# Feed-forward transposes moved from TensorE to VectorE squares and DMA, with the next input loaded most of a block sooner

## The chip, the cores and the metric

The kernel runs on one core of a Trainium2 chip. The metric is the device time of one execution, in microseconds (us). Five engines work side by side: TensorE (PE, matrix products), VectorE (DVE), ScalarE (ACT), GpSimd (POOL) and SyncE (SP), which here issues the transfers (DMAs). They meet through semaphores. SBUF is the working memory with 128 partitions; PSUM holds what PE produces.

## The reference

64 sequences of 64 tokens with 256 features (x, 4096 tokens in all) pass through four layers. Each has parameters that depend on a condition vector of the sequence (cond, 64 numbers).

- Layer 0: an up projection with GELU gate, quantised activations and ternary weights.
- Layer 1: attention with 16 heads and a gated feed-forward part, each behind a conditional root-mean-square norm:
```
x = x + a_alpha * _attention(_ada_rmsnorm(x, t, gamma, beta), W_q, W_k, W_v, W_o)
return x + f_alpha * _swiglu(_ada_rmsnorm(x, t, gamma, beta), gate_w, hidden_w, out_w, out_b)
# _ada_rmsnorm: (t @ gamma_w.T) * x * rsqrt(mean(x*x) + eps) + (t @ beta_w.T)
# _swiglu: silu(x @ gate_w.T) * (x @ hidden_w.T) @ out_w.T + out_b, with 1024 hidden units
```
- Layer 2: a layer norm over the 256 features with weight, bias and a conditional term.
- Layer 3: an adapter with matrices of its own for each sequence, 256 to 128 and back:
```
down = relu(einsum('bld,bnd->bln', x, Wd + dWd[b]) + bd)
return x + einsum('bln,bdn->bld', down, Wu + dWu[b]) + bu
```
The change lies in the stretch that computes the feed-forward part of layer 1, layer 2 and layer 3.

## The kernel before

The 4096 tokens are 8 blocks (i = 0 to 7) of 512 tokens, each 4 tiles of 128. Layer 0 and the attention come first; the sum after the attention, x2, is written to DRAM (x2d). The last loop, `for n in range(5, N)`, begins at about 447 us of the span. Step n is block i = n // 8 and part f = n % 8: 128 of the 1024 hidden units. Products of full precision are made from a high and a low half (three matmuls, mm3, L83 to L85).

A block has two layouts. Token-major has 128 tokens on the partitions: there the norms' means are taken and the residual is added. Feature-major has 128 features on the partitions (two chunks c of 256): products need their input so. The turn from the first to the second happens at two places of the loop, and PE makes it, as four transposes of 128 x 128 into a PSUM bank each time:

- norm_turn, for the normed input xn of the next block, chunk c at f = 5 and 6. Transposes (L256), then DVE multiplies by gamma (xg, L259), POOL adds beta (L260), and one step later split makes the halves xh (ACT, L239) and xl (POOL, L240).
- f_adapt, for the layer norm's output x3 of the block before, chunk c at f = 4 and 5. Transposes (L913), then DVE makes x4 (L914), the adapter's input.

One step of the loop, in order: f_inner (PE: gate and value products into two banks; ACT: silu, L796; DVE: their product sg, L799); the pieces of other blocks; f_parts (ACT: high half hhi, L836; DVE: low half hlo, L837); f_outer for the step two before (PE: acc += h x wout, L83 to L85).

The pieces of other blocks, by f: 0: the load of x2 of block i+1 (f_load, fx, L759, 512 KB). 1: its squares (f_begin: ACT junkf L232, POOL root L223 and L225); of block i-1 acc times alpha plus x2 (f_scaled L859, f_added L864) and its statistics. 2: f_center (DVE nm L876, ACT x3 L878); the rows of alpha and out_b for block i (f_rows, L271, four transfers). 3: f_scale, xn from x2 and the root (ACT xnf, L247). 6: the load of the adapter's down matrices wd (L890, four transfers). 7: of wu (L894, four); f_down of block i-1 (PE L943, ACT Relu dn L947); f_up of block i-2 (PE L959 in two chunks, DVE yo L975, store out_y L977); on POOL f_common (the shared part of wd, L904) and f_base (x2 plus out_b, L780).

PSUM has eight banks here: four with the tag gh, two mm, two acc. At f = 7 the mm banks are taken in the order up chunk 0, down, up chunk 1, so up chunk 1 takes the bank that yo of up chunk 0 reads. Of the SBUF tiles that count here, x1 (x2 and x3 of a block) has five buffers, xn one, xh and xl two each, x4 two, dn and yo one.

Order: PE, ACT, DVE and POOL follow the order in which the program is written (`tc.manual_schedule`). SP's transfers are placed by a planner. Every transfer on SP also waits for the one that stands eight before it.

Of the kernel before, what the change touches and what calls it, by code (L numbers as in the profile page):

```python
# [8 lines left out]
F32 = mybir.dt.float32  # L9
# [3 lines left out]
ALU = mybir.AluOpType  # L13
# [4 lines left out]
P = 128  # L18
NB = 64
L = 64  # L20
D = 256
NTOK = NB * L
T = 512
NBLK = NTOK // T
BB = T // L
TT = T // P
# [6 lines left out]
V_NORM, V_AG, V_AB, V_AA, V_FG, V_FB, V_FA, V_LIN = range(8)  # L33
# [3 lines left out]
def tile_kernel(ctx: ExitStack, tc, xT, x, condT, cw, upT, downT, qkvT, woT, ghT, outT_w,  # L37
                vecs, rows, g1, g2, gb, out):
    nc = tc.nc
# [3 lines left out]
    main = ctx.enter_context(tc.tile_pool(name="main", bufs=1))  # L43
# [8 lines left out]
    pools = {}  # L52
# [7 lines left out]
    uid = [0]  # L60

    def bank(tag):
        uid[0] += 1
        tags = pools["tags"]
        if tag not in tags:
            tag = "mm"
        return pools["ps"].tile([P, 512], F32, tag=tag, bufs=tags[tag], name=f"{tag}_{uid[0]}")
# [19 lines left out]
    def b3(ap):  # L87
        return ap.rearrange("p (b l) -> p b l", l=L)
# [19 lines left out]
    E = mybir.EngineType  # L108
    engines = {E.PE, E.Activation, E.DVE, E.Pool}
    ordered = ExitStack()  # L110
# [19 lines left out]
    def bc(v, c, i, bs=slice(0, BB)):  # L130

        n = bs.stop - bs.start
        return cv[:, v, c, i * BB + bs.start:i * BB + bs.stop].unsqueeze(2).broadcast_to([P, n, L])
# [87 lines left out]
    def rsqrt(ss, scale, eps, name, n=TT):  # L221
        ms = main.tile([P, TT], F32, tag="ms", bufs=2, name=f"ms_{name}")
        nc.gpsimd.tensor_scalar(ms[:, :n], ss, scale, eps, ALU.mult, ALU.add)  # L223
        rs = main.tile([P, TT], F32, tag="rs", bufs=2, name=f"rs_{name}")
        nc.gpsimd.tensor_tensor(rs[:, :n], ms[:, :n], nhalf[:, :n], ALU.pow)  # L225
        return rs
# [11 lines left out]
    def split(hl, c, xs, eng=None):  # L238
        nc.scalar.copy(hl[0][:, c], xs)  # L239
        (eng or nc.vector).tensor_tensor(hl[1][:, c], xs, hl[0][:, c].bitcast(F32), ALU.subtract)  # L240
# [11 lines left out]
    def norm_turn(xn, hl, i, c, vg, vb):  # L252

        pt = bank("mm")
        for t in range(TT):
            nc.tensor.transpose(pt[:, t * P:(t + 1) * P], xn[:, t, c * P:(c + 1) * P], ident)  # L256
        uid[0] += 1
        xg = main.tile([P, T], F32, tag="xg", bufs=2, name=f"xg{uid[0]}")
        nc.vector.tensor_tensor(b3(xg), b3(pt), bc(vg, c, i), ALU.mult)  # L259
        nc.gpsimd.tensor_tensor(b3(xg), b3(xg), bc(vb, c, i), ALU.add)  # L260
        return lambda: split(hl, c, xg, nc.gpsimd)

# [494 lines left out]
    def f_load(i):  # L757
        x2 = block(f"fx2_{i}")
        nc.sync.dma_start(out=x2, in_=tok(x2d, i))  # L759
        fblk[i] = dict(x2=x2)  # L760

    def f_begin(i):
        fblk[i]["rs"] = rms(fblk[i]["x2"], f"f{i}")

    def f_scale(i):
        fblk[i]["n"] = norm_tm(fblk[i]["x2"], fblk[i]["rs"], f"f{i}", True)
# [26 lines left out]
    def f_inner(n):  # L793
        pg, pv = f_products(n)
        sg = main.tile([P, T], F32, tag="st", bufs=2, name=f"sg{n}")
        nc.scalar.activation(sg, pg, AF.Silu)  # L796
        if n == LAST:
            return sg, pv
        nc.vector.tensor_tensor(sg, pv, sg, ALU.mult)  # L799
        return sg  # L800
# [15 lines left out]
    def f_parts(n, sg):  # L816
        pool = pools["b"]
        if n in KEPT:

            if n == KEPT[0]:  # L820
                fun["kept"] = parts("kept")
            h_hi, h_lo = (k[:, n - KEPT[0]] for k in fun["kept"])
        else:
            h_hi = pool.tile([P, T], F32R, tag="oh", bufs=3, name=f"hhi{n}")
            h_lo = pool.tile([P, T], F32R, tag="ol", bufs=3, name=f"hlo{n}")
        fun[n] = (h_hi, h_lo)
        if n == LAST:
            sg, pv = sg
            halves = [slice(k * T // 2, (k + 1) * T // 2) for k in range(2)]
            for k in halves:  # L830
                nc.vector.tensor_tensor(sg[:, k], pv[:, k], sg[:, k], ALU.mult)
                nc.scalar.copy(h_hi[:, k], sg[:, k])
            for k in halves:
                nc.vector.tensor_tensor(h_lo[:, k], sg[:, k], h_hi[:, k].bitcast(F32), ALU.subtract)  # L834
            return
        nc.scalar.copy(h_hi, sg)  # L836
        nc.vector.tensor_tensor(h_lo, sg, h_hi.bitcast(F32), ALU.subtract)  # L837
# [69 lines left out]
    def f_adapt(i, c):  # L907
        B = fblk[i]
        if c == 0:
            B["x4"] = pools["c"].tile([P, 2, T], F32, tag="x4", bufs=2, name=f"x4_{i}")  # L910
        pt = bank("mm")
        for t in range(TT):
            nc.tensor.transpose(pt[:, t * P:(t + 1) * P], B["x3"][:, t, c * P:(c + 1) * P], ident)  # L913
        nc.vector.scalar_tensor_tensor(b3(B["x4"][:, c]), b3(pt), w2[:, c:c + 1], bc(V_LIN, c, i),  # L914
                                       ALU.mult, ALU.add)

    def f_turn(i, k):
# [16 lines left out]
    def f_down(i, half=None):  # L934
        B = fblk[i]
        if half in (None, 0):
            B["dn"] = pools["c"].tile([P, T], F32, tag="dn", bufs=1, name=f"dn{i}")
        b0, b1 = (0, BB) if half is None else (half * BB // 2, (half + 1) * BB // 2)
        pd = bank("mm" if half is None else "acc")
        for b in range(b0, b1):  # L940
            for c in range(2):
                for s in range(2):
                    nc.tensor.matmul(pd[s * 64:(s + 1) * 64, (b - b0) * L:(b - b0 + 1) * L],  # L943
                                     lhsT=B["wd"][b // 4][:, b % 4, c, s * 64:(s + 1) * 64],
                                     rhs=B["x4"][:, c, b * L:(b + 1) * L], start=c == 0, stop=c == 1,
                                     tile_position=(0, 64 * s))
        nc.scalar.activation(B["dn"][:, b0 * L:b1 * L], pd[:, :(b1 - b0) * L], AF.Relu, bias=vc[:, 5, 0:1])  # L947
# [211 lines left out]
    bias = pools["bias"] = pools["c"].tile([P, 2, D], F32, name="bias")  # L1159
    gbt = pools["c"].tile([P, 4, D], F32, tag="yo", bufs=1, name="gbt")  # L1160
    nc.sync.dma_start(out=gbt, in_=gb)
    late = []
    for n in range(5, N):
        i, f = divmod(n, 8)
        more = i + 1 < NBLK

        for rest in late:
            rest()
        late = []
        if i > 0 and f == 2:  # L1170
            f_added(i - 1, 1)
            f_stats(i - 1, 1)
            rln = rsqrt(fblk[i - 1]["mv"][:, :, 1], 1.0, 1e-5, f"ln{i - 1}")
        sg = f_inner(n)
        if i > 0 and f in (4, 5):
            f_adapt(i - 1, f - 4)
        if more and f in (5, 6):
            late = [norm_turn(*fblk[i + 1]["n"], i + 1, f - 5, V_FG, V_FB)]
        up = i - 2 if more and f == 7 else i - 2 if not more and f == 0 else -1
        if up >= 0:  # L1180

            def between(pus):
                f_up_store(up, pus, chunks=range(1))
                if more:
                    f_down(i - 1)
            pus = f_up_products(up, between=between)
            f_up_store(up, pus, chunks=range(1, 2))
        elif more and i > 0 and f == 7:
            f_down(i - 1)
        f_parts(n, sg)  # L1190
        if n > 5:
            f_outer(n - 2, range(2 if n - 2 in KEPT else TT))
        if n == 6:
            for k in range(2):
                nc.vector.scalar_tensor_tensor(bias[:, k], gbt[:, 2 * k + 1], 0.1, gbt[:, 2 * k], ALU.mult, ALU.add)
        if i > 0:
            if f == 1:
                for k in range(2):
                    f_scaled(i - 1, k)
                f_added(i - 1, 0)  # L1200
                f_stats(i - 1, 0)
            if f == 2:
                f_center(i - 1, range(TT), rln)
        if i > 0 and more:
            if f == 0:
                f_load(i + 1)
            if f == 1:
                f_begin(i + 1)
            if f == 3:
                f_scale(i + 1)  # L1210
        if f == 2 and i > 0:
            f_rows(i)

        if f == (6 if more else 1):
            f_weights(i, "wd")
        if f == (7 if more else 1):
            f_weights(i, "wu")
        if more and f == 7:
            f_common(i, "wd", 0)
            f_base(i)  # L1220
        if i > 0 and f == 0:
            f_common(i - 1, "wd", 1)
        if i > 0 and f in (3, 4):
            f_common(i - 1, "wu", f - 3)
        if not more:
            if f == 4:
                f_base(i)
            if f in (5, 6):
                f_common(i, "wd", f - 5)
                f_common(i, "wu", f - 5)  # L1230
# [57 lines left out]
```

## Time and profile before

| | |
|---|---|
| time, median of 3 runs | 748.66 us (748.53 to 748.88) |
| the profiled execution | 748.95 us, span 746.8 us |
| last loop, f = 0 of block 1, 2, 3, 4, 5, 7 on PE | 458.95, 496.41, 535.73, 575.08, 614.47, 693.07 us |
| DMA traffic over the span | 159 GB/s on average |

Times in the profile are us from the start of the span unless marked ns. A group line reads: line, engine, operation, out<-in, shapes, count, then busy time and mean ns of one instruction, then the idle time before them with what ended it. A timeline line reads: start, duration, engine, line, operation, out<-in, shapes, count, and in brackets the idle time just before with its releaser. SPq marks the issue of transfers: its time is the time on SP, not until the data land. PEclk is the clock that TensorE was granted, as a share of full speed.

The shares of the chain that ended last, by engine:

```profile
PE 61%; DVE 17%; ACT 11%; issue 5%; DMA 3%; POOL 2%; SPq 1%; DVEq 0%; ACTq 0%; POOLq 0%
```

Most of what the end waited for is PE's own work.

### The profile page before, as it was taken

How to read it: one execution, taken by the hardware profiler on the slowest of the kernel's cores; microseconds unless marked ns; L12 is line 12 of the kernel's file. 1: busy time of each engine (PE TensorE's matmuls, PEld its weight loads, DVE VectorE, ACT ScalarE, POOL GpSimd, SP SyncE). 2: the span in 40 equal slices, each digit the busy share in tenths (PEclk: the TensorE clock that was granted, in tenths of full speed). 3: DMA queues.
4: the chain of work that ended last, by engine and by line, in shares of the span. 5: the costliest groups of instructions: out<-in, count | busy, mean ns of one | idle time of the engine just before them, and what ended most of it. 6: DMA issues, size and time to landing. Idle time of an engine off the chain costs nothing.

```text
span 746.8 us, 17456 instructions
## 1 busy us (share of the span) xinstructions
PE 734.7 (98%) x7036; PEld 612.1 (82%) x7036; DVE 542.2 (73%) x843; ACT 405.6 (54%) x849; POOL 340.4 (46%) x359
## 2 busy tenths in 40 slices
PE   9999999999999999999999999999999999999997
PEld 8866766777686878888888888888888888888886
DVE  4998878867687698889888876646555555565676
ACT  5553445335435588998888674535253434434242
POOL 2123133133134426765655427464646464545292
PEclk9999999999999999999999999999999999999999
DMA  8897999999995866444655237623261709080821
GB/s 258 244 265 171 270 280 231 300 278 261 229 273 108 195 153 162 113 134 122 164 150 129 79 101 183 148 52 91 63 163 32 196 4 224 1 198 2 222 62 58
DMA packets 117456, 118.87 MB, mean 159 GB/s; under 512 B 39632, under 2 KB 101200, under 8 KB 117376
## 3 DMA queue, kind: packets, MB, share of 16 engines
q1 hardware_dynamic: 109232, 91.29, 49.6%
q0 software_dynamic: 7488, 25.37, 10.9%
q10 hardware_dynamic: 656, 1.11, 0.5%
q8 instruction: 55, 0.90, 0.5%
q14 instruction: 25, 0.20, 0.1%
HBM read 71.41 MB, written 29.56 MB: 135 GB/s over the span
## 4 chain that ended last, share of the span: by engine, by line
PE 61%; DVE 17%; ACT 11%; issue 5%; DMA 3%; POOL 2%; SPq 1%; DVEq 0%; ACTq 0%; POOLq 0%
PE mm L83 9%; PE mm L85 8%; PE mm L84 8%; PE gh L85 4%; PE gh L84 4%; PE gh L83 4%; PE mm L476 3%; PE mm L298 3%; PE acc L83 2%; DMA wu<-s2d 2%; PE S L649 2%; DVE sg L799 2%; PE acc L85 2%; PE acc L84 2%; ACT x L878 2%
## 5 line engine op out<-in xcount | busy, mean ns | idle before, releaser
L83 PE MATMUL mm<-up,xhl 128*128 128x512 f32 x240 | 97.2, 405 | 0.0
L83 PE MATMUL gh<-xhf,gh 128*128 128x512 f32 x244 | 95.2, 390 | 0.0
L85 PE MATMUL gh<-xhf,gh 128*128 128x512 f32 x244 | 95.2, 390 | 0.0
L84 PE MATMUL gh<-xlf,gh 128*128 128x512 f32 x244 | 95.1, 390 | 0.0
L85 PE MATMUL mm<-up,xll 128*128 128x512 f32 x240 | 93.9, 391 | 0.0
L84 PE MATMUL mm<-up,xhl 128*128 128x512 f32 x240 | 93.6, 390 | 0.0
L799 DVE TENSOR_TENSOR sg<-gh,sg 128x512 f32<-128x512 f32 x60 | 41.3, 688 | 70.7 <-ACT sg L796 37.9
L450 ACT ACTIVATE g<-mm,rs_l 128x512 f32<-128x512 f32 x64 | 43.8, 689 | 80.6 <-PE mm L85 48.1
L837 DVE TENSOR_TENSOR hlo<-sg,hhi 128x512 fp32r<-128x512 f32 x58 | 55.2, 951 | 30.4 <-ACT hhi L836 29.5
L836 ACT CAST hhi<-sg 128x512 fp32r<-128x512 f32 x58 | 36.0, 620 | 71.9 <-DVE sg L799 71.1
L83 PE MATMUL acc<-wout,hhi 128*128 128x256 f32 x248 | 71.9, 290 | 0.0
L85 PE MATMUL acc<-wout,hlo 128*128 128x256 f32 x248 | 69.5, 280 | 0.8 <-DVE hlo L834 0.6
L451 DVE SCALAR_TENSOR_TENSOR h<-mm,rs_l,g 128x512 f32<-128x512 f32 x64 | 46.4, 744 | 32.8 <-PE mm L85 29.7
L84 PE MATMUL acc<-wout,hhi 128*128 128x256 f32 x248 | 69.3, 279 | 0.0
L260 POOL TENSOR_TENSOR xg<-xg,cv 128x512 f32<-128x512 f32 x32 | 35.3, 1114 | 71.2 <-DVE xg L259 71.2
L83 PEld LDWEIGHTS mm<-up,xhl 128*128 128x128 f32 x240 | 45.1, 188 | 15.2 <-issue 2.4
L85 PEld LDWEIGHTS gh<-xhf,gh 128*128 128x128 f32 x244 | 45.8, 188 | 9.6
L85 PEld LDWEIGHTS mm<-up,xll 128*128 128x128 f32 x240 | 45.0, 188 | 10.1
L84 PEld LDWEIGHTS mm<-up,xhl 128*128 128x128 f32 x240 | 45.2, 188 | 8.5
L83 PEld LDWEIGHTS gh<-xhf,gh 128*128 128x128 f32 x244 | 45.8, 188 | 7.3
L84 PEld LDWEIGHTS gh<-xlf,gh 128*128 128x128 f32 x244 | 45.8, 188 | 7.3
L660 DVE TENSOR_REDUCE mx<-S 128x16 f32<-128x1024 f32 x32 | 39.0, 1220 | 17.3 <-PE S L649 17.3
(220 smaller groups left out, 1929.6 us busy)
## 6 DMA issues: line engine op xcount, KB each, us to landing
gt<-in_g SPq DMA_DIRECT2D x32, 512.0 KB, 9.1
rows<-alphad SPq DMA_DIRECT2D x48, 256.0 KB, 4.8
vb<-vx SPq DMA_DIRECT2D x32, 256.0 KB, 5.1
wd<-s1d SPq DMA_DIRECT2D x32, 256.0 KB, 6.2
wu<-s2d SPq DMA_DIRECT2D x32, 256.0 KB, 6.0
xt<-in_x SPq DMA_DIRECT2D x8, 512.0 KB, 7.6
s1d<-stgs POOLq DMA_DIRECT2D x16, 256.0 KB, 8.0
s1d<-stg POOLq DMA_DIRECT2D x16, 256.0 KB, 7.9
```

The source lines that it names most:

```text
L83: nc.tensor.matmul(out, lhsT=l[0], rhs=r[0], start=first, stop=False)
L84: nc.tensor.matmul(out, lhsT=l[0], rhs=r[1], start=False, stop=False)
L85: nc.tensor.matmul(out, lhsT=l[1], rhs=r[0], start=False, stop=last)
L260: nc.gpsimd.tensor_tensor(b3(xg), b3(xg), bc(vb, c, i), ALU.add)
L298: nc.tensor.matmul(pb[s][c * 64:(c + 1) * 64], lhsT=gl[h], rhs=gt[h, c * GC:(c + 1) * GC], start=True, stop=True, tile_position=(64 * s, 6 ...
L450: nc.scalar.activation(g, pg, AF.Gelu, scale=rs[:, t:t + 1])
L451: nc.vector.scalar_tensor_tensor(h[:, ch * 512:(ch + 1) * 512], pv, rs[:, t:t + 1], g, ALU.mult, ALU.mult)
L476: nc.tensor.matmul(py[:, :D], lhsT=qt[:, f, :], rhs=wq[:, f, :], start=f == 0, stop=f == 7)
L660: nc.vector.tensor_reduce(ms, sv, AX.X, ALU.max)
L799: nc.vector.tensor_tensor(sg, pv, sg, ALU.mult)
L836: nc.scalar.copy(h_hi, sg)
L837: nc.vector.tensor_tensor(h_lo, sg, h_hi.bitcast(F32), ALU.subtract)
```

## The change

Both turns leave PE, except for xn of block 1 and x3 of the last block.

- A new function spread turns a 128 x 1024 tile in two steps. One DVE instruction transposes every 32 x 32 square in place of its own (nc.vector.transpose into the tile turned). Then 16 transfers on SP, each 32 partitions x 8 pieces x 32 numbers (32 KB in pieces of 128 bytes), put the squares where the feature-major layout has them.
- spread(xn of block i+1) stands at the end of f = 0 (i = 1 to 6), spread(x3 of block i-1) at f = 3 after f_inner (i = 1 to 7): 13 in all, 208 transfers.
- norm_spread does what norm_turn does after its transposes, from the spread tile in SBUF. It stands where norm_turn stood. f_adapt reads the spread tile too; both its chunks now stand at f = 7 ahead of f_inner.
- f_load, f_begin and f_scale are no longer those of block i+1 at f = 0, 1 and 3, but those of block i+2 at f = 4 (5 in block 0), 6 and 7.
- From the loop on, SP too follows the written order.

```
+    def spread(src, name):
+        turned = pools["b"].tile([P, 16, L], F32, tag="ex2", bufs=2, name=f"turned_{name}")
+        nc.vector.transpose(turned.rearrange("p a l -> p (a l)").rearrange("p (c t x) -> p c t x", c=2, t=TT),
+                            src.rearrange("p t (c x) -> p c t x", c=2))
+        xt = pools["b"].tile([P, 2, 512], F32, tag="pts", bufs=2, name=f"spread_{name}")
+        blocks = turned.rearrange("p (n m) (h r) -> p n m h r", m=2, h=2)
+        for k in range(4):
+            for q in range(4):
+                m, h = divmod(q, 2)
+                nc.sync.dma_start(
+                    out=xt[32 * q:32 * q + 32].rearrange("p c (t r) -> p (c t) r", t=TT)[:, :, 32 * k:32 * k + 32],
+                    in_=blocks[32 * k:32 * k + 32, :, m, h])
+        return xt
+
+    def norm_spread(xt, hl, i, c, vg, vb):
...
+        nc.vector.tensor_tensor(b3(xg), b3(xt[:, c]), bc(vg, c, i), ALU.mult)
+        nc.gpsimd.tensor_tensor(b3(xg), b3(xg), bc(vb, c, i), ALU.add)
+        return lambda: split(hl, c, xg, nc.gpsimd)
...
     def f_adapt(i, c):
-        pt = bank("mm")
-        for t in range(TT):
-            nc.tensor.transpose(pt[:, t * P:(t + 1) * P], B["x3"][:, t, c * P:(c + 1) * P], ident)
-        nc.vector.scalar_tensor_tensor(b3(B["x4"][:, c]), b3(pt), w2[:, c:c + 1], bc(V_LIN, c, i),
+        nc.vector.scalar_tensor_tensor(b3(B["x4"][:, c]), b3(B["spread"][:, c]), w2[:, c:c + 1], bc(V_LIN, c, i),
                                        ALU.mult, ALU.add)
...
+    ordered.close()
+    ordered.enter_context(tc.manual_schedule(engines=engines | {E.SP}))
...
+        if i > 0 and f == 7:
+            for c in range(2):
+                f_adapt(i - 1, c)
         sg = f_inner(n)
-        if i > 0 and f in (4, 5):
-            f_adapt(i - 1, f - 4)
         if more and f in (5, 6):
-            late = [norm_turn(*fblk[i + 1]["n"], i + 1, f - 5, V_FG, V_FB)]
+            xn, hl = fblk[i + 1]["n"]
+            if i == 0:
+                late = [norm_turn(xn, hl, i + 1, f - 5, V_FG, V_FB)]
+            else:
+                late = [norm_spread(fblk[i + 1]["turned"], hl, i + 1, f - 5, V_FG, V_FB)]
...
+        if i > 0 and f == 3:
+            fblk[i - 1]["spread"] = spread(fblk[i - 1]["x3"], f"x3_{i - 1}")
         f_parts(n, sg)
...
-        if i > 0 and more:
-            if f == 0:
-                f_load(i + 1)
-            if f == 1:
-                f_begin(i + 1)
-            if f == 3:
-                f_scale(i + 1)
+        if i + 2 < NBLK:
+            if f == (4 if i > 0 else 5):
+                f_load(i + 2)
+            if f == 6:
+                f_begin(i + 2)
+            if f == 7:
+                f_scale(i + 2)
+        if i > 0 and more and f == 0:
+            fblk[i + 1]["turned"] = spread(fblk[i + 1]["n"][0], f"xn{i + 1}")
```

More of the change, by code (lines that the diff above doesn't have):

```diff
@@ L259, in norm_turn @@
         nc.vector.tensor_tensor(b3(xg), b3(pt), bc(vg, c, i), ALU.mult)
+        nc.gpsimd.tensor_tensor(b3(xg), b3(xg), bc(vb, c, i), ALU.add)
[14 more added lines that the diff above has]
+    def norm_spread(xt, hl, i, c, vg, vb):
+        uid[0] += 1
+        xg = main.tile([P, T], F32, tag="xg", bufs=2, name=f"xg{uid[0]}")
+        nc.vector.tensor_tensor(b3(xg), b3(xt[:, c]), bc(vg, c, i), ALU.mult)
         nc.gpsimd.tensor_tensor(b3(xg), b3(xg), bc(vb, c, i), ALU.add)
```

## The prediction

> **What bounds the kernel now.** I read the engine totals first, then windows of single blocks of the last loop, then what TensorE (PE) waits for, then the timelines of a block.
>
> ```profile
> PE 734.7 (98%) x7036; PEld 612.1 (82%) x7036; DVE 542.2 (73%) x843; ACT 405.6 (54%) x849; POOL 340.4 (46%) x359
> ```
> The windows view of three blocks (length in us, busy time and count of each engine, PE clock, DMA share, GB/s):
> ```profile
> core 0: us, PE busy (x) PEld busy (x) DVE busy (x) ACT busy (x) POOL busy (x), PEclk, DMA share, GB/s
> 496.41:535.73 39.32, 39.03 (x338) 34.53 (x337) 22.15 (x36) 16.57 (x35) 22.98 (x21) 1.00 0.27 68
> 535.73:575.08 39.35, 39.05 (x338) 34.56 (x337) 22.55 (x36) 16.57 (x35) 21.11 (x19) 1.00 0.43 108
> 653.75:693.07 39.32, 39.03 (x339) 34.52 (x338) 22.55 (x36) 16.57 (x35) 21.08 (x19) 1.00 0.40 95
> ```
> PE is busy 39.0 of 39.3 us at full clock. DVE, ACT, POOL and the transfers have half the block free. PE's waits after 440 us are 3.2 us in all:
> ```profile
> PE mm L256 <- DVE x L914: 1.8, 6, 0.3
> PE gh L925 <- ACT x L878: 0.8, 2, 0.6
> PE acc L85 <- DVE hlo L834: 0.6, 1, 0.6
> ```
> So PE time taken out is time won, as long as what replaces it is early enough. The last of these waits is in the tail, where DVE is late.
>
> **What is removed.** One steady block (i=3, begins at 535.73) on PE:
> ```profile
> 555.01 0.60 PE L913 MATMUL mm<-ident,x 128*128 128x128 f32 x4
> 555.36 0.36 PE L83 MATMUL acc<-wout,hhi 128*128 128x256 f32 x1
> 559.57 0.60 PE L913 MATMUL mm<-ident,x 128*128 128x128 f32 x4
> 560.46 0.63 PE L256 MATMUL mm<-ident,xnf 128*128 128x128 f32 x4 [0.30 <-DVE x L914]
> 560.85 0.36 PE L83 MATMUL acc<-wout,hhi 128*128 128x256 f32 x1
> ```
> Start to next start, a group of four costs 0.35 (555.01 to 555.36), 0.89 with its wait (559.57 to 560.46) and 0.39 (560.46 to 560.85); the fourth group is 0.36, and each leaves the next product some 0.06 late: 2.2 us a block. Six blocks (i=1 to 6) lose all four groups, i=7 loses two (0.85): 6 x 2.2 + 0.85 = 14.1 us. A block without stalls would last 39.35 - 2.2 = 37.1 us, and 748.95 - 14.1 = 734.8 is the floor.
>
> **What is added.** Thirteen DVE transposes of 128x1024 and 208 DMAs of 32 KB on SP. DVE rows of that size:
> ```profile
> L662 DVE TENSOR_TENSOR ex<-S,mx 128x1024 f32<-128x1024 f32 x32 | 39.2, 1225 | 1.1
> L460 DVE TENSOR_SCALAR h<-h,am 128x1024 f32<-128x1024 f32 x32 | 24.2, 755 | 1.1
> ```
> I take 1.2 us (bounds 0.75 to 2.4, double the slower row, because the write is permuted). The transpose of xn, at f=0, lies in DVE's free time and costs nothing; that of x3 lies on the path below.
>
> No row of before has a DMA on 32 partitions. SP's rows nearest to it:
> ```profile
> 431.23 0.38 SPq L759 DMA_DIRECT2D fx<-x2d  x1
> 431.66 0.50 SPq L1161 DMA_DIRECT2D gbt<-in_gb  x1
> 445.12 1.25 SPq L271 DMA_DIRECT2D rows<-alphad  x2
> 448.22 2.92 SPq L894 DMA_DIRECT2D wu<-s2d  x4
> 580.30 3.15 SPq L890 DMA_DIRECT2D wd<-s1d  x4
> ```
> A transfer on all 128 partitions takes SP 0.38 to 0.50 us; rows and wu, on 64 partitions and in 256 pieces each as here, 0.62 (1.25/2) and 0.73 (2.92/4); wd behind others 0.79 (3.15/4). Likest in partitions and pieces are rows, so I take a pitch of 0.65 us, bounds 0.36 and 0.80. Sixteen are 10.4 us of SP. SP is now in program order, so this burst holds up what stands behind it.
>
> **The steady block in the new order**, with zero at PE's start of f=0. ACT's centring of x3 ends at 19.2 (554.98 in this block):
> ```profile
> 552.90 2.08 ACT L878 ACTIVATE x<-x,nm,rs_ln 128x256 f32<-128x256 f32 x4 [1.93 <-DVE nm L876]
> 554.88 0.58 ACT L796 ACTIVATE sg<-gh 128x512 f32<-128x512 f32 x1
> 568.02 0.62 ACT L239 CAST xhf<-xg 128x512 fp32r<-128x512 f32 x1 [1.09 <-POOL xg L260]
> ```
> The spread of x3 stands behind f=3's gate product on DVE, which ends at 20.4. The transpose ends at 21.6. SP is free by then: its spread of xn (f=0) ran from 6.7 to 17.1, its rows to 19.7. Sixteen issues at 0.65 end at 32.0. The last square lands some 1.9 us after its issue began (out_y, 128 KB, lands in 1.8, the nearest row), so at 33.3. DVE makes x4 from it, two of L914's 0.74: 34.85. The down product, which PE could start at 32.6 (f=7's products run 28.9 to 31.6, the first up chunk to 32.6), starts at 34.85: a PE wait of 2.2.
>
> Behind the burst stands fx of block i+2, whose load the change puts at f=4. It is issued at 32.1 although f=4 begins on PE at 16.5. Its landing takes 3.7 us from an idle queue (fx's least; median 7.1): 35.85. Behind that wait stand on ACT, in its written order: four squares of junkf with their reads (2.14 us, from 544.12 to 546.26 in this block) to 38.0, the cast xhf of chunk 1 to 38.6, and silu of f=7 to 39.15. Then DVE: sg(7) to 39.85 and, after it, yo of the first up chunk to 40.55. This last frees the PSUM bank which the second up chunk needs (mm has two banks: up, down, up). So PE does its second up chunk at 40.6 instead of after the down product (36.7): a wait of 3.85. With 1.0 for that chunk and 1.4 for the outer product the next block begins at 43.1. In short P = 32.8 + 16p for a pitch p; it equals today's 39.35 at p = 0.41.
>
> The other edits. DVE now reads xt in SBUF where it read PSUM: I cost that at nothing, bounds 0 and +0.9 an instruction (hlo takes 0.69 alone and 1.57 beside POOL); 17 free us of DVE a block cover it, except in x4, where it would add up to 1.8 to the 34.85 and then changes only the first of the two waits. POOL's root of fx (0.45 + 1.02) starts at 38.0 instead of in f=1; ACT's four xnf (1.71), behind hhi(7), end at about 42.2, ahead of the next silu (about 44.5): hidden, and without that cover 2 us a block. wd, now behind fx on SP, is issued at 32.5 to 34.5 and lands at about 40.7 (its median is 6.2 from issue); POOL's two pairs of adds behind it (2.52 and 2.53) end at 45.8, ahead of the next block's L864 (after 47): hidden, by little; if it is missed, x3 and everything above shift by the same amount. out_y and wu follow yo and have a block's time until their use. The spread of xn has landed by 19.0; its reader on DVE stands behind sg of f=5, at about 24: hidden until p passes 0.95.
>
> **Sum.** Blocks i=2 to 5: 4 x (43.1 - 39.35) = +15.1. Block i=1 has no up product; there the late cast delays xl of chunk 1 (POOL, 1.29 us) to 40.8, in the middle of the next f=0: 39.98 against 37.46, +2.5. Block i=6 loads no fx: only the x4 wait, 37.1 + 2.2 = 39.3, 0. In i=7 x4 (now at f=7 instead of f=4 and 5, where DVE had it at 718.43 and 721.37) comes at about 728.7, and its two ops push DVE's last sg and hlo, on which the tail waits already: +2.5 less 0.85 removed, +1.7. Together +19.3: 748.95 + 19.3 = 768. The profiled execution is 0.29 above the median 748.66, and 2.15 of it lies outside the span.
>
> **The skill weighed.** The Trainium skill, "DMA: Bandwidth & Descriptors", section "Rules for kernel authors", says to join many small transfers, since under 64 KB one pays mostly overhead; these are 32 KB. The rows above say the same with SP's pitch. An estimate with that page's fixed 2 us or so a transfer, one after another, would be 16 x 2 = 32 us a spread and a block of over 60 us; rows and wu show transfers overlapping, so I stay with the pitch. "TensorE: Matmul & The Clock Gate", Part 1, says that a PE gap over about 3.4 us halves the clock for about as long; no row of before shows such a gap. By it, as an estimate, each of four blocks would lose up to 1.7 us more, 775 in all.
>
> **Rivals.**
> A, ends faster: 32-partition DMAs issue like fx's (0.36). For: fx and gbt; against: rows and wu. P = 38.6, 4 x -0.8; i=1 and i=6 lose nothing but the transposes, -2 each, i=7 -0.85: about 741, with 0.33 some 739, never under 734.8. It decides below a pitch of 0.41.
> B, only the x4 wait counts: ACT's junkf does not hold silu(7), because fx lands before 31.6 or the order differs. Against: the SP order puts fx behind the burst. 39.3 a block, and +1.7 in the tail: 750.6.
> C, longer: p = 0.8 gives 45.6, +6.3 for 4 blocks, 2.4 more than above in each of the other three (+5, +2, +4): 748.95 + 25 + 11 = 785; or fx takes 5.7 us as behind two rows: +2 for 5 blocks, 778.
>
> **How the numbers follow.** The forecast (both waits, p 0.6 to 0.7, 762 to 775) 0.50; C 0.21; A 0.15; B 0.12; the rest 0.02 at no difference. Range: A and the top of C left out, 747 to 787. A measurement tells 0.2% (1.5 us) from none. Faster: A and a little of B, 0.16; within: 0.04; slower 0.80.
>
> **What would show it.** PE's waits: L943 for DVE's x4 some 2.2 us, L959 for DVE's yo some 3.9, four or more times; ACT's L232 idle for the DMA of fx; sixteen SP issues over about 10 us; blocks of 43 us in the middle, 39 for i=6. Wrong, if the 16 issues take under 6.5 us, if fx is issued ahead of them, or if transposes of 128x1024 take over 3 us.

## The result and the profile after

The changed kernel takes 784.4 us (median of 4 runs, 783.2 to 785.7), the kernel before 748.8 beside it: a ratio of 1.047 (95% interval 1.045 to 1.050). It is slower by 35.7 us. The profiled execution has 785.74 us and a span of 783.9.

The engine totals and the chain by engine, of the changed kernel:

```profile
PE 741.4 (95%) x6932; PEld 617.0 (79%) x6932; DVE 555.5 (71%) x856; ACT 405.9 (52%) x849; POOL 338.5 (43%) x359
PE 45%; DVE 20%; ACT 12%; SPq 9%; issue 6%; DMA 6%; POOL 2%; DVEq 0%; ACTq 0%; POOLq 0%
```

PE has 104 instructions fewer and is busy longer (741.4 against 734.7). In the chain, SP's issuing and the transfers hold 15% where they held 4%. The windows of blocks i = 2, 3, 5 and 6:

```profile
core 0: us, PE busy (x) PEld busy (x) DVE busy (x) ACT busy (x) POOL busy (x), PEclk, DMA share, GB/s
500.11:545.67 45.56, 39.84 (x322) 35.32 (x321) 25.50 (x38) 18.24 (x40) 26.39 (x23) 0.94 0.47 109
545.67:592.39 46.72, 41.79 (x321) 36.91 (x321) 24.68 (x37) 16.14 (x35) 19.87 (x19) 0.87 0.49 112
637.82:684.69 46.87, 41.63 (x321) 36.73 (x321) 24.55 (x37) 15.98 (x35) 19.75 (x19) 0.87 0.48 110
684.69:724.40 39.71, 37.57 (x323) 33.22 (x321) 24.34 (x38) 13.99 (x26) 18.80 (x16) 1.00 0.52 117
```

Blocks 2 to 5 have grown from 39.3 us to between 45.4 and 46.9, and block 1 from 37.5 to 41.6; block 6, which loads no fx, hardly has. The clock, 1.00 before, is 0.87 to 0.94 in the long ones: that is why PE is busy longer with fewer instructions. PE's waits from 440 us on:

```profile
PE mm L963 <- issue: 14.0, 6, 3.6
PE mm L979 <- DVE yo L995: 12.1, 4, 3.9
PE acc L83 <- ACT hhi L855: 4.6, 1, 4.6
PE mm L963 <- DVE x L934: 1.1, 4, 0.3
```

The first line names no engine ("issue"); it is the down product's wait for x4, whose end stands in DVE's row below. The second is the second up chunk's wait for yo. Block 2's chain of both, from the timelines of SP, DVE, ACT and PE (the block begins at 500.11):

```profile
506.58 10.44 SPq L273 DMA_DIRECT2D spread_xn<-turned_xn  x16
517.12 3.65 SPq L294 DMA_DIRECT2D rows<-alphad  x4
522.04 10.44 SPq L273 DMA_DIRECT2D spread_x<-turned_x  x16
532.57 0.55 SPq L782 DMA_DIRECT2D fx<-x2d  x1
...
520.78 1.23 DVE L266 STREAM_TRANSPOSE turned_x<-x 128x1024 f32<-128x1024 f32 x1
533.97 1.41 DVE L934 SCALAR_TENSOR_TENSOR x<-spread_x,w,cv 128x512 f32<-128x512 f32 x2 [3.82 <-DMA spread_x<-turned_x]
...
536.47 0.42 ACT L232 ACTIVATE junkf<-fx 128x256 f32<-128x256 f32 x1 [7.05 <-DMA fx<-x2d]
539.01 0.59 ACT L819 ACTIVATE sg<-gh 128x512 f32<-128x512 f32 x1
...
534.82 0.34 PE L963 MATMUL mm<-x,wd 128*64 128x64 f32 x4 [1.81 <-issue]
535.43 1.97 PE L963 MATMUL mm<-x,wd 128*64 128x64 f32 x60 [0.28 <-DVE x L934]
541.03 1.23 PE L979 MATMUL mm<-dn,wu 128*64 128x64 f32 x18 [3.63 <-DVE yo L995]
```

The transpose takes 1.23 us. Sixteen issues take 10.44 us, 0.65 each. fx, written at f=4, is issued at 532.57, after f=7 has begun on PE (529.05). ACT, idle for 7.05 us, squares it from 536.47 on, and only then comes silu of f=7 (539.01). PE waits 1.81 + 0.28 us for x4 and 3.63 us for yo. Block 4 runs the same way (1.41 + 0.28 and 3.86 us). Blocks 3 and 5 do not. Block 3 on SP and PE:

```profile
568.11 11.66 SPq L273 DMA_DIRECT2D spread_x<-turned_x  x16
...
581.96 4.08 PE L963 MATMUL mm<-x,wd 128*64 128x64 f32 x64 [2.56 <-issue]
588.28 1.98 PE L979 MATMUL mm<-dn,wu 128*64 128x64 f32 x32 [2.23 <-DVE yo L995]
```

Its burst of sixteen issues takes 11.66 us, because one of them takes 1.56 us (in block 5 11.63 us, with one of 1.78; why is not known). PE waits 2.56 us for x4 (2.72 in block 5), the clock falls to 0.50 already there, the down product takes 4.1 us instead of 2.6, and 2.23 us (2.38) are left of the wait for yo. The two windows after block 2's second wait, with columns as above (the second up chunk; the outer product), show the price that the forecast's sum did not hold:

```profile
541.03:542.94 1.91, 1.91 (x32) 1.79 (x32) 0.00 (x0) 0.00 (x0) 1.91 (x3) 0.50 0.36 137
542.94:545.67 2.73, 2.73 (x14) 2.73 (x13) 1.91 (x2) 2.61 (x6) 2.73 (x3) 0.50 0.26 96
```

At clock 0.50 they take 1.91 and 2.73 us. Before, with clock 1.00, the same work took 1.03 and 1.48 us, from the start of one of these lines to the next (the second up chunk, the outer product, the next block):

```profile
572.57 1.10 PE L959 MATMUL mm<-dn,wu 128*64 128x64 f32 x32
573.60 0.39 PE L83 MATMUL acc<-wout,hhi 128*128 128x256 f32 x1
575.08 0.39 PE L83 MATMUL gh<-xhf,gh 128*128 128x512 f32 x1
```

### The profile page after: what moved, and what is told of

It reads as the page before. It is cut to its first block, busy times and chain, and to the rows that moved or that the text cites. A ratio compares the mean times of both kernels' runs of the same rounds, so it can differ in the third digit from the quotient of the medians.

```text
span 783.9 us, 17525 instructions
## 1 busy us (share of the span) xinstructions
PE 741.4 (95%) x6932; PEld 617.0 (79%) x6932; DVE 555.5 (71%) x856; ACT 405.9 (52%) x849; POOL 338.5 (43%) x359
## 3 DMA queue, kind: packets, MB, share of 16 engines
q0 software_dynamic: 7488, 25.37, 10.4%
## 4 chain that ended last, share of the span: by engine, by line
PE 45%; DVE 20%; ACT 12%; SPq 9%; issue 6%; DMA 6%; POOL 2%; DVEq 0%; ACTq 0%; POOLq 0%
SPq L273 8%; PE mm L83 7%; PE mm L85 7%; PE mm L84 7%; PE mm L499 3%; PE mm L321 3%; DVE sg L822 2%; PE gh L84 2%; PE gh L85 2%; PE gh L83 2%; DMA fx<-x2d 2%; PE S L672 2%; PE acc L83 2%; DVE h L474 2%; PE mm L979 2%
## 5 line engine op out<-in xcount | busy, mean ns | idle before, releaser
L83 PE MATMUL acc<-wout,hhi 128*128 128x256 f32 x248 | 73.7, 297 | 4.6 <-ACT hhi L855 4.6
L859 ACT CAST hhi<-sg 128x512 fp32r<-128x512 f32 x58 | 35.9, 620 | 78.5 <-DVE sg L822 77.8
L860 DVE TENSOR_TENSOR hlo<-sg,hhi 128x512 fp32r<-128x512 f32 x58 | 55.2, 952 | 28.0 <-ACT hhi L859 27.0
L85 PE MATMUL acc<-wout,hlo 128*128 128x256 f32 x248 | 72.0, 290 | 0.2 <-DVE hlo L860 0.2
L84 PE MATMUL acc<-wout,hhi 128*128 128x256 f32 x248 | 72.1, 291 | 0.0
L83 PEld LDWEIGHTS acc<-wout,hhi 128*128 128x128 f32 x248 | 49.3, 199 | 7.6 <-ACT hhi L855 4.8
L85 PEld LDWEIGHTS gh<-xhf,gh 128*128 128x128 f32 x244 | 46.1, 189 | 9.8
L84 PEld LDWEIGHTS mm<-up,xhl 128*128 128x128 f32 x240 | 45.2, 188 | 8.5
L819 ACT ACTIVATE sg<-gh 128x512 f32<-128x512 f32 x61 | 36.1, 591 | 29.8 <-PE gh L85 29.8
```

Of the source, the lines that this page charges most:

```text
L83: nc.tensor.matmul(out, lhsT=l[0], rhs=r[0], start=first, stop=False)
L84: nc.tensor.matmul(out, lhsT=l[0], rhs=r[1], start=False, stop=False)
L85: nc.tensor.matmul(out, lhsT=l[1], rhs=r[0], start=False, stop=last)
```

## The experiments

The theory after this reading: the 16 issues of a spread hold SP for 10.4 us, which delays x4 and fx, each of which stops PE at f=7; the clock then falls; the tail is late through x4 on DVE. Rivals: the small pieces themselves are slow on the DMA engines; the early load and its place in ACT's order cost by themselves; PE's slow products have another reason than the clock.

### Four wide transfers for sixteen narrow ones

```
-        for k in range(4):
-            for q in range(4):
-                m, h = divmod(q, 2)
-                nc.sync.dma_start(out=xt[32 * q:32 * q + 32]...[:, :, 32 * k:32 * k + 32],
-                                  in_=blocks[32 * k:32 * k + 32, :, m, h])
+        for k in range(4):
+            m, h = divmod(k, 2)
+            nc.sync.dma_start(out=xt...[:, :, 32 * k:32 * k + 32], in_=blocks[:, :, m, h])
```

> The changed kernel with each spread made of 4 transfers on 128 partitions (1024 pieces of 128 bytes, 128 KB each) in place of 16 on 32 partitions: the same bytes and pieces, a quarter of the issues. Left out: the squares stay in their own group of 32 partitions, so x4 and xg are not true transposes; the work is otherwise the same. Theory (SP's time for 16 issues is the cause): a burst of about 2 to 2.6 us, x3 landed by about 27, fx issued at about 25, no wait at f=7, clock 1.00, blocks of about 37.1 us, tail as before the change: 735 to 738. Rival (the pieces of 128 bytes themselves are what is slow, on the DMA engines): the landing takes 8 us or more from the first issue, waits at f=7 stay, 760 or more.

Measured: 740.9 us (ratio 0.989, interval 0.986 to 0.992); no wait of PE at f=7 in the middle blocks. The kernel leaves the squares in their groups of partitions, so it is a test of the time and no replacement. A middle block and block 7 with the tail, in the windows view:

```profile
532.60:569.72 37.12, 37.12 (x322) 33.02 (x321) 25.86 (x38) 16.57 (x36) 20.88 (x19) 1.00 0.62 143
681.44:738.20 56.76, 49.61 (x546) 44.05 (x544) 36.97 (x61) 15.23 (x28) 27.09 (x23) 0.97 0.47 117
```

In the timelines, SP in that middle block and DVE in the tail:

```profile
554.24 2.82 SPq L272 DMA_DIRECT2D spread_x<-turned_x  x4
557.15 0.63 SPq L781 DMA_DIRECT2D fx<-x2d  x1
...
715.08 3.43 DVE L933 SCALAR_TENSOR_TENSOR x<-spread_x,w,cv 128x512 f32<-128x512 f32 x2
718.44 0.74 DVE L853 TENSOR_TENSOR sg<-gh,sg 128x256 f32<-128x256 f32 x2
```

One issue of 128 partitions and 1024 pieces takes 0.70 us (2.82/4), one of 32 partitions and 256 pieces 0.65: the price is per issue, not per byte or piece. With four issues the block is 37.12 us, the forecast's 37.1 without stalls. The rival of slow pieces falls. The time misses the expected 735 to 738 through the second window: 56.8 us where the kernel before has 53.7 (746.8 - 693.07). There x4's data have long landed, but its two operations take 3.43 us (1.40 in the middle blocks) beside POOL's adds, and stand ahead of the last sg. PE waits 3.2 us behind them.

### fx ahead of the burst

```
-            if f == (4 if i > 0 else 5):
+            if f == (2 if i > 0 else 5):
                 f_load(i + 2)
```

> The changed kernel with fx of block i+2 issued on SP at f=2, ahead of rows and of the spread of x3; nothing else moved. Theory (two waits at f=7, both from SP's burst of 16 issues, and the clock drop that the longer one brings): the wait of L979 for yo (12.1 us in 4 blocks) goes, the wait of L963 for x4 stays at about 2.3 us a block (fx's 0.55 and more of SP time now stands ahead of the burst, so some 0.6 later), the clock stays at 1.00 in the middle blocks, which last about 39.5 to 40 instead of 46; the tail is unchanged. 784.4 - 4 x 6.5 = 758, 755 to 762. Rival (the wait of x4 alone stretches the block, fx's lateness is hidden behind it): block no shorter than 45, 780 or more.

Measured: 765.2 us (ratio 1.022, interval 1.019 to 1.025). yo's wait is gone, x4's stays. A middle block in the windows view:

```profile
540.99:582.30 41.31, 39.18 (x323) 34.81 (x321) 24.64 (x38) 16.56 (x36) 20.35 (x19) 0.96 0.54 128
```

So the second wait, with what followed it, cost some 5 us a block (46.1 to 41.1), and the rival, that x4's wait alone stretches the block, falls. The block is 1.5 us longer than expected: after the waits of 1.5 to 2.2 us in blocks 2 to 5 the clock is lower too, and the down product takes 3.5 to 3.8 us. In block 6, where the clock stayed whole after a wait of 1.61 us, it takes 2.4. The two windows (block 3, block 6):

```profile
575.78:579.58 3.80, 3.52 (x65) 3.38 (x66) 1.82 (x3) 0.00 (x0) 1.98 (x2) 0.60 0.91 281
699.09:701.51 2.42, 2.13 (x65) 2.00 (x66) 1.83 (x3) 0.00 (x0) 0.82 (x1) 1.00 0.96 279
```

### The squares behind silu

```
-            if f == 6:
-                f_begin(i + 2)
             if f == 7:
-                f_scale(i + 2)
+                f_begin(i + 2)
         if i > 0 and more and f == 0:
+            f_scale(i + 1)
```

> The changed kernel with the squares of fx of block i+2 (junkf) at the end of f=7 instead of f=6, so behind silu of f=7 in ACT's order, and xnf at f=0 of the next block, ahead of the spread; fx is still loaded at f=4, behind the burst. Theory (fx's late landing costs only through silu of f=7, which stands behind junkf): the wait of L979 for yo goes, the wait of L963 for x4 stays at about 2 us, blocks as in e1_fx_first (about 41), 784.4 - 4 x 5.2 - 0.4 = 763, 761 to 768. Rival (fx's transfer meets the last squares' transfers and makes x4 late by itself, or POOL's root then holds up x2 plus out_b): blocks of 44 or more, 775 or more.

Measured: 771.3 us (768.7 to 774.0). Here fx lands as late as in the changed kernel, and yo's wait is gone all the same, so fx does its harm through ACT's order. The time is above the expected range. The blocks i = 2 to 4 in the windows view differ by their clock:

```profile
500.21:539.97 39.76, 37.58 (x322) 33.26 (x321) 23.82 (x37) 15.73 (x32) 21.45 (x18) 1.00 0.51 111
539.97:582.87 42.90, 40.33 (x322) 35.87 (x321) 23.96 (x38) 16.70 (x38) 22.12 (x18) 0.92 0.54 126
582.87:624.76 41.89, 39.33 (x322) 34.76 (x321) 25.18 (x38) 16.27 (x34) 21.44 (x18) 0.96 0.57 126
```

The first, where the clock stayed whole after a wait of 1.9 us, lasts 39.76 us: close to what rival B gave for x4's wait alone (39.3). The others are 2 to 3 us longer, after waits of 2.44 and 2.29 us. Block 6 of this run has a wait of 1.90 us as well, and there the clock fell to 0.54 over the down product.

### Products without use in the waits

```
+    def filler(i, dst, count):
+        for _ in range(count):
+            nc.tensor.matmul(dst, lhsT=gh[0][:, 0, :P], rhs=xh[:, 0], start=True, stop=True)
...
+        filler(i + 1, pd, 7 if i > 0 else 15)      # ahead of the down product
+        filler(i, fun["early"][0], 16)             # ahead of the second up chunk
```

> The changed kernel with extra products without use on PE in its two waits of f=7: 7 (15 in block 1) ahead of the down product, into its bank before it starts, and 16 after it, into the first gh bank of the next step; their results are written over. Nothing that waits is moved. Theory (the waits are 3.6 to 4 us by themselves, and the rest of a block's loss is the halved clock after them): PE clock 1.00 in the middle blocks, blocks of about 43.2 us (the forecast's P) against 46.1, block 1 about 39.5 against 41.55, so 784.4 - 4 x 2.9 - 2 = 771, 768 to 774. Rival (the slow products after the waits are slow for another reason, such as operands that compete for SBUF): no shorter than 783.

Measured: 778.2 us (775.9 to 780.4), above the expected range. The two runs lie 4.4 us apart, and the profiled one has lost 4.7 us before the last loop, where nothing was changed, so I compare from block 1 on. From its start to that of block 7 the filled kernel takes 257.1 us, the changed one 265.8. Blocks 3 to 5 take 132.4 against 139.0, 2.2 us less each. Block 2 gains only 0.4 us (45.2 against 45.6): PE waits 1.07 us there for POOL's xl. Block 3 in the windows view (block 4 is alike):

```profile
548.45:592.89 44.44, 43.44 (x346) 37.47 (x345) 25.44 (x38) 16.68 (x36) 20.39 (x18) 1.00 0.51 119
```

The clock stays at 1.00 and the block comes within 1.3 us of the forecast's 43.1, although work was added and nothing else moved. So the clock is a cause by itself, in these blocks of 2.2 us of the 3 that the forecast lacked; the expected 2.9 was too much.

The same in the variant with fx first, with 7 products in the one wait that is left:

> The variant with fx issued ahead of the spread (e1_fx_first), with 7 products without use on PE (15 in block 1) in the wait that is left, ahead of the down product and into its bank; their results are written over. Theory (in e1 the blocks last 41 instead of 39.4 because the clock falls even after a wait of 1.6 to 1.9 us, and the down product then runs at 0.6): clock 1.00 in the middle blocks, down product 2.0 to 2.3 us instead of 3.5 to 3.8, blocks of 39.4 (39.2 to 39.8), so 765.2 - 4 x 1.7 - 1.5 = 757, 755 to 760. Rival (the down product is slow because its operands come late or compete, not through the clock): down product 3.5 us or more, 763 or more.

Measured: 762.5 us (762.0 to 763.0), less of a gain than expected. Clock 1.00, down product 2.3 to 2.4 us: that part holds. But the middle blocks last 39.4, 40.2, 40.9 and 39.9 us, 40.1 in the mean against 41.15 (the mean of 41.04, 41.31, 40.95 and 41.32): in two of them PE still waits 0.52 and 1.27 us for x4 after the filler. About 1 us of each of those blocks is the clock. x4 comes unevenly because the burst of x3 is uneven: it takes 10.44 us in block 2 and 11.38 in block 3, and in block 4, after a burst of 10.66, DVE can start on x4 only 2.9 us after its end (1.4 to 1.6 in the others). Why was not tried.

### x3 on PE, in one block and in all

In block 7 alone (x3 of block 6 turned by PE at f=4 and 5):

> The changed kernel with x3 of block 6 (needed in block 7) turned by PE at f=4 and 5, as in the kernel before; all else as changed. Theory (the tail's loss is x4 standing on DVE, waiting for its transfers, ahead of the last sg and hlo): block 7 and the tail take 53.7 us again instead of 59.5, and 784.4 - 5.8 = 778.6, 777.5 to 780. Rival (the tail is late because of what earlier blocks pushed into it, POOL's adds or wu and wd): no shorter than 783.

Measured: 781.7 us (781.3 to 782.1), above the expected range. Block 7 and the tail in the windows view:

```profile
724.26:779.50 55.24, 48.86 (x554) 43.36 (x552) 35.57 (x60) 15.34 (x28) 27.51 (x24) 1.00 0.42 111
```

They take 55.2 us here and 59.5 in the changed kernel (783.9 - 724.40). So in the profiled executions 4.3 of the 5.8 us that were expected are x4's place, and the rest is not; between the medians the gain is 2.8 us (784.44 and 781.68).

In all blocks, so that only xn goes by squares and transfers:

> The changed kernel with x3 turned by PE at f=4 and 5 in all blocks, as in the kernel before; xn still goes by squares and transfers, fx is still loaded a block sooner. Theory (only the burst of x3 holds up f=7; the spread of xn, at f=0, is hidden): no waits at f=7, blocks i=1 to 6 shorter than before by the two xn groups and the wait between them, about 1.1 to 1.2 us each, tail as before: 748.8 - 6.9 = 742, 741 to 744. Rival (the early load with its squares ahead of silu costs by itself, or DMA traffic of the xn squares does): 748 or more.

Measured: 742.9 us (741.3 to 743.4; ratio 0.992, interval 0.990 to 0.993), as expected. A middle block in the windows view:

```profile
532.43:570.42 37.99, 37.99 (x331) 33.77 (x329) 22.45 (x37) 16.57 (x36) 21.31 (x19) 1.00 0.51 126
```

The timelines of SP and DVE in it:

```profile
538.87 10.43 SPq L273 DMA_DIRECT2D spread_xn<-turned_xn  x16
549.40 2.61 SPq L294 DMA_DIRECT2D rows<-alphad  x4
552.10 0.56 SPq L782 DMA_DIRECT2D fx<-x2d  x1
...
557.79 0.68 DVE L282 TENSOR_TENSOR xg<-spread_xn,cv 128x512 f32<-128x512 f32 x1
```

The same burst of 10.4 us costs nothing here. It ends at 549.3, and its reader on DVE (the last line) starts at 557.79, 25 us into the block.

### The order alone

The kernel before, with SP in the written order and fx loaded, squared and scaled at the change's places; no spread:

```
+    ordered.enter_context(tc.manual_schedule(engines=engines | {E.SP}))
...
-                f_load(i + 1)   # f = 0; f_begin at 1, f_scale at 3
+                f_load(i + 2)   # f = 4; f_begin at 6, f_scale at 7
```

> The kernel before, all transposes on PE, with only two things of the change: SP in the written order in the last loop, and fx of block i+2 loaded at f=4, squared at f=6, scaled at f=7. Theory (the new places do no harm without the burst ahead of them): within 1 us of the kernel before, 748 to 750. Rival (junkf ahead of silu of f=7 in ACT's order, or POOL's root ahead of wd and fx's base, costs at f=7): a wait of 1 us or more a block, 753 or more.

Measured: 746.6 us (745.9 to 747.5; ratio 0.997, interval 0.996 to 0.998), blocks of 38.83 us, below the expected 748 to 750. The early load does no harm without the burst; it even wins 0.5 us a block. PE's two groups of transposes of f=5:

```profile
558.84 0.60 PE L913 MATMUL mm<-ident,x 128*128 128x128 f32 x4
559.27 0.60 PE L256 MATMUL mm<-ident,xnf 128*128 128x128 f32 x4
```

They start 0.43 us apart where the kernel before had 0.89 with a wait of 0.30, which is most of the gain. The likely reason: ACT's four xnf (1.71 us), which stood ahead of silu of f=4, have moved, and x4 comes sooner. The rival of the order falls. Of the 1.36 us a block that turning xn by squares won above (39.35 to 37.99), 0.5 is therefore the early load's.

### The adapter one step later

The burst is kept. fx goes ahead of it, x3 of block 6 goes by PE, and x4, down and up move to f=0 of the next block:

```
-            if f == (4 if i > 0 else 5):          # f_load(i + 2)
+            if f == (2 if i > 0 else 5):
-        if i > 0 and f == 7:                       # f_adapt(i - 1, c), both chunks
+        if i > 1 and f == 0:                       # f_adapt(i - 2, c)
-        up = i - 2 if more and f == 7 else i - 2 if not more and f == 0 else -1
+        up = i - 3 if f == 0 else i - 2 if not more and f == 4 else -1
-                    f_down(i - 1)
+                    f_down(i - 2)
```

> The changed kernel with three moves: fx of block i+2 issued at f=2 ahead of rows and spread; x4, the down product of block i-1 and the up product of block i-2 one step later, at f=0 of the next block (block 5's up product at f=4 of block 7); x3 of block 6 turned by PE. Theory (the burst hurts only where something needs it at f=7): x3 lands at about 35, x4 is needed at about 39, no wait in the middle blocks, clock 1.00, blocks of 37.1 us, tail as before: 748.8 - 6 x 2.2 = 735.6, 734 to 738. Rival (the burst or the piled-up SP order then delays something else, such as the next spread of xn or rows, which stand behind wu in SP's order): waits at f=5 or f=1 and 742 or more.

Measured: 749.0 us (747.0 to 750.4; ratio 1.000, interval 0.999 to 1.001). The middle blocks last 37.13 to 37.33 us, as expected, with no waits; the gain is lost in block 7. SP and POOL there, from their timelines:

```profile
705.78 2.62 SPq L917 DMA_DIRECT2D wu<-s2d  x4
708.50 2.57 SPq L294 DMA_DIRECT2D rows<-alphad  x4
...
717.08 2.99 POOL L803 TENSOR_TENSOR fx<-fx,rows 128x512 f32<-128x512 f32 x2 [14.65 <-DMA rows<-alphad]
731.29 0.19 POOL L223 TENSOR_SCALAR ms_ln<-bmv 128x2 f32<-128x2 f32 x1
```

wu of block 7 waits for the buffer that block 5's up product frees, which I had put at f=4, and rows stand behind it on SP. POOL's adds then run until 731, the root of the layer norm starts behind them, and PE waits 6.0 us. So I moved that up product to f=1:

```
-        up = i - 3 if f == 0 else i - 2 if not more and f == 4 else -1
+        up = i - 3 if f == 0 else i - 2 if not more and f == 1 else -1
```

> The variant with x4, down and up one step later (e7_later), with one more move: block 5's up product in block 7 at f=1 instead of f=4, so that wu of block 7, and rows behind it on SP, no longer wait for it until f=4. Theory (e7's lost 12 us lie in block 7 alone: rows were issued at 708.5, so POOL's x2 plus out_b began at 717.1 and the last root of the layer norm came 6 us late): blocks of 37.1 us as in e7_later, no wait of 6 us before the last transposes, the tail 53.7 us plus 3.9 us for the products moved into it: span about 735, time 737, 735 to 740. Rival (the tail is late through DVE or POOL work that the shorter blocks push into it): 743 or more.

Measured: 739.4 us (739.3 to 740.9; ratio 0.986, interval 0.983 to 0.988): the best of all, 1.4% faster than the kernel before, with 12 of the 13 spreads and their 16 transfers each kept. The windows of a middle block and of block 7 with the tail:

```profile
602.15:639.32 37.17, 37.17 (x323) 32.97 (x322) 25.30 (x37) 16.47 (x36) 20.53 (x19) 1.00 0.64 142
676.45:738.60 62.15, 53.43 (x682) 46.87 (x680) 35.85 (x64) 16.10 (x30) 30.97 (x26) 1.00 0.45 120
```

Its tail is 62.15 us, 4.5 above the expected 57.6. A wait of 2.2 us for the centred x3 is left there, so the rival has a share in it.

## Why the prediction was right, and where it fell short

The forecast was 768 (747 to 787), slower with a chance of 0.80. It came out slower, at 784.4: right in sign and mechanism, inside the range near its top, and 16 us short in size. That the range held it is luck in part. The forecast's own band was 762 to 775; the range went higher for rival C, which gave 785, and C's conditions did not come about: the pitch was 0.65 us and not 0.8 (0.73 in the two long bursts), and fx landed in 4.0 us and not 5.7. By the steps of the prediction:

- The terms that it bounded were measured as taken: transpose 1.2 (1.23), pitch 0.65 (0.65), landing of a square 1.9 (median 1.9), fx's landing 3.7 (3.9 to 4.1; from 532.57 to 536.47 in block 2). The floor of 37.1 us a block was measured as 37.12 with four issues.
- The two waits were as predicted in blocks 2 and 4: 2.2 us for x4 (2.1 and 1.7), 3.85 for yo (3.63 and 3.86). In blocks 3 and 5 x4's was longer (2.56 and 2.72) and yo's shorter (2.23 and 2.38). Taking yo's wait away left x4's, in two ways.
- "With 1.0 for that chunk and 1.4 for the outer product the next block begins at 43.1" is the step that failed. It put the clock at nothing. At half the clock these took 1.91 and 2.73 us in block 2, and the next f=0 lost some 0.8 as well (3.55 against 2.73); in blocks 3 and 5 the down product was slow too. The blocks i=2 to 5 lasted 184.6 us in all where the forecast had 172.4: 12.2 of the 17.5 us by which the profiled execution lies above the sum (785.74 and 768.25). The filled waits return 2.2 us in each of blocks 3 to 5; of the remaining 0.8 the cause was not taken apart.
- The forecast had named this price, as an estimate of up to 1.7 us a block from the skill, and left it outside the sum because no row of before showed a long wait of PE. It was right about the direction and too small.
- Block 1 lost 1.6 us more than predicted (41.55 against 39.98), and not at the predicted place: PE does not wait for xl at the start of block 2. The down product starts 36.0 us into the block instead of 34.85, after a wait of 3.61 us, and at a clock of 0.75 it takes 3.2 us instead of 2.0.
- "+1.7" for block 7 was mis-sized: +5.8. The data of x4 came 35.9 us into the block (760.27 - 724.40), as forecast (728.7 - 693.07 = 35.6), but its two operations took 2.58 us there instead of the 1.5 that I took (two of 0.74), beside POOL's adds. The forecast's cover for DVE's reads from SBUF (DVE's free time) does not exist in the tail. The last sg then began at 762.8, 38.4 us into the block, instead of 34.3 before, and PE waited 4.6 us behind it.
- Block 6, predicted at 39.3, took 39.7.
- Rival A is refuted by the pitch. Rival B's block was seen as 39.76 us, where nothing but x4 was late and the clock stayed whole.

The Trainium skill, "TensorE: Matmul & The Clock Gate", Part 1, puts the fall of the clock at waits of over about 3.4 us. Here it fell after 3.6 to 3.9 us, as the page has it, but after shorter waits too. In the last loops of all the profiled executions, and among waits of PE of over 1 us that began at full clock, the clock stayed at 1.00 after those of up to 1.41 us and was lower after all of 2.29 us or more; of the fourteen between 1.54 and 2.25 us it fell after seven. What decides between these was not found. The measurements decide: a wait of under 2 us can cost the clock. "DMA: Bandwidth & Descriptors", section "Rules for kernel authors", speaks against many transfers under 64 KB. It holds here for the queue that issues them (0.65 us each at 32 KB, 0.70 at 128 KB) and not for their landing (1.9 us each): they overlap, and a late enough reader does not notice them.

## What to carry to other kernels

Work taken from the bounding engine is a gain only where its replacement is in time: price a train of small transfers by issues times the queue's pitch, and then look at what is written behind it on that queue and behind the consumers of that on the other engines. A late load does harm through the instruction that waits for it at the head of an in-order queue, so move the load ahead of the train, or the waiting instruction behind the urgent one. Add to every new wait of TensorE the clock that may fall after it.

## What the runs showed that was not expected

- SP takes 0.65 us for an issue of 32 partitions in 256 pieces and 0.70 for one of 128 partitions in 1024 pieces: a transfer four times as large costs it nearly the same.
- Two x4 operations on DVE that read SBUF take 1.40 us in the middle blocks, and 2.58 and 3.43 us in tails where POOL adds beside them.
- Loading and scaling the next input a block sooner, with SP in the written order and nothing else, gained 0.3%, probably through ACT work that moved out of the way of a silu.
- The clock of PE fell to 0.60 over the product after a wait of 1.85 us (the variant with fx first), and stayed at 1.00 after one of 1.90 (the first block shown of the variant with late squares); after another of 1.90 in that same run it fell to 0.54.
- Sixteen equal issues on SP do not always take the same time: 10.44 us in block 2 of the changed kernel, 11.66 and 11.63 in blocks 3 and 5, where a single issue took 1.56 and 1.78 us instead of 0.61.
